# A two-layer decoder on one core: where a second group's norm stands in layer 0, and where the first root and the gathered sums stand in layer 1

## The chip, the cores and the metric

The kernel runs on one core of one Trainium2 chip. The metric is device time in microseconds (us), the median of three runs. A profile is one further execution, recorded by the hardware profiler.

The engines are called as the profile calls them: PE (TensorE, matmuls and transposes, with PEld for its weight loads), DVE (VectorE), ACT (ScalarE), POOL (GpSimd) and SP (SyncE, which here only issues transfers). Each engine works through its own queue in order and waits where an instruction needs another engine's result.

## What is computed

The reference is a decoder with two layers on 32 sequences of 100 tokens, 256 values a token. Each layer adds three blocks to the tokens, each behind a layer norm:

```python
x = x + _L0_attn_ref(_layernorm(x), Wq, Wk, Wv, Wo, bq, bk, bv, bo)   # causal softmax attention, 16 heads of 64
x = x + _L0_xattn_ref(_layernorm(x), ctx_512, ...)                    # cross attention to 361 context rows
x = x + _L0_ffn_ref(_layernorm(x), ...)                               # shared MLP + 8 experts, 2 per token
x = x + _L1_attn_ref(_layernorm(x), W1, b1, W2, b2)                   # causal attention without softmax, heads of 16
x = x + _L1_xattn_ref(_layernorm(x), ctx_512, ...)                    # cross attention, 16 heads of 64
x = x + _L1_ffn_ref(_layernorm(x), ...)                               # shared MLP + 64 experts, 8 per token

def _layernorm(x, eps=1e-5):
    m = mean(x); v = var(x)
    return (x - m) / sqrt(v + eps)
```

Everything is float32.

## The kernel before

The 3200 tokens lie in on-chip memory as 25 tiles of 128 tokens (`self.x`). A sequence is called a batch, so batch b holds tokens 100 b to 100 b + 99 and straddles tiles. The six blocks run one after the other, and each hands its successor normed tokens in transposed form (`self.xnT`).

**Queues.** PE's instructions stand in the order in which the program emits them (`tc.manual_schedule`). The queues of the other engines are ordered by a planner at build time, which may move an instruction ahead of others where its inputs allow it; `self.depend(got, [other], reason)` ties an instruction behind another one. All matmul results of the two attention blocks go to eight PSUM banks used in turn; a bank is free again once its result has been copied out.

**A norm** is made in groups of tiles. `norm_stats(f, groups)` (L163 on) takes the statistics of tile f (L175, L178); with the last tile of a group come the addition of epsilon (L180), the square root on ACT (L181) and the reciprocal on DVE (L182) for the whole group. `norm_rows` then forms the normed rows on DVE (L185), remembers the last one as `self.last_row`, and adds a bias to x on POOL (L200); `norm_turn` transposes them on PE (L207) and copies the result into `xnT`, by `evac`. `evac` (L124 on) counts its calls and sends each second copy to ACT (L128), the others to DVE (L129); its argument `act_of` changes the share: with 1, all go to ACT.

**Layer 0's attention.** SP loads the first tiles of x, then the weights wq and wk, then tiles 4 to 7, biases, wv, wo and the rest. `front(f)` norms and transposes a group (tiles 0 to 3, 4 to 7 and so on). `proj(b0, c, ...)` makes two of eight chunks of q (copied out with a scaled bias on ACT, L299) or k (DVE, L301) for two batches, `vals` the values of a batch in two halves. Then follow 64 steps, two a batch: scores, projections for the batches to come, the transposes of the step before, values. Scores are masked and reduced on DVE, exponentiated on ACT (L330) and scaled on POOL (L334).

**Layer 0's experts leave their rows in memory** (`y_d`). Layer 1 picks them up: `gather0(pool, f)` fetches two rows for each token of tile f by two indirect transfers, which POOL issues (L1252), into eight buffers `yk`, and adds each to x with its weight on DVE (L1257, "gathered sums" below). With `after` given, both sums stand behind that instruction.

**Layer 1's attention** begins with the gathers of tiles 0 to 3 and their statistics. To give PE work in the meantime, `ahead(steps, n)` makes keys and values of the cross attention that comes next (`keys1`: one step is two matmuls and two copies of 361 columns; `vals1`: a half of a batch is three of 512 columns); the text calls this the fill. The first group is tiles 0 to 3, the later ones three tiles each (FRONT1). Ahead of the loop stand the fill, the first two groups' norms and the projections of the first four batches. A step of the loop is one batch: `scores` (16 small matmuls in four banks, masked on DVE, L999), a projection, `vals` (L980), `values` of the batch before (L1009), the output projection of a finished tile (L237). In three of four steps a tile of a group to come is gathered and its statistics are taken; in the fourth the group is normed and transposed.

Of the kernel before, what the change touches and what calls it, by code (L numbers as in the profile page):

```python
# [12 lines left out]
AF = mybir.ActivationFunctionType  # L13
# [64 lines left out]
class Kernel:  # L78
    def __init__(self, ctx, tc, a):
        self.ctx, self.tc, self.nc, self.a = ctx, tc, tc.nc, a  # L80
        nc = tc.nc
        self.n_evac = 0
        self.const = ctx.enter_context(tc.tile_pool(name="const", bufs=1))
        self.wts = ctx.enter_context(tc.tile_pool(name="wts", bufs=1))
        self.lnp = ctx.enter_context(tc.tile_pool(name="ln", bufs=2))
        self.norms, self.norm_of = {}, {}
        self.x = self.const.tile([P, NF, D], F32, tag="x", name="x_sb")
        xd = a["x"].rearrange("b t d -> (b t) d").rearrange("(f p) d -> p f d", p=P)

        def load_x(f, n=4):  # L90
            n = min(n, NF - f)
            nc.sync.dma_start(self.x[:, f : f + n, :], xd[:, f : f + n, :])

        self.load_x = load_x
        load_x(0, 2)
        load_x(2, 2)
        self.xnT = self.const.tile([P, NK, NT], F32, tag="xnT", name="xnT")
        self.ident = self.const.tile([P, P], F32, tag="ident", name="ident")
        make_identity(nc, self.ident)
# [63 lines left out]
    def norm_stats(self, f, groups, after=None):  # L163

        nc = self.nc
        f0 = max(g for g in groups if g <= f)
        n, i = groups[f0], f - f0
        if i == 0:
            self.norm_of[n] = [
                self.lnp.tile([P, n, *k], F32, tag=f"{tag}{n}", name=tag)  # L170
                for tag, k in (("st", [6]), ("mv", [2]), ("rstd", []))
            ]
        st, mv, rstd = self.norm_of[n]
        self.norms[f] = mv[:, i, 0:1], rstd[:, i : i + 1]
        got = nc.vector.bn_stats(st[:, i, :], self.x[:, f, :])  # L175
        if after is not None:
            self.depend(got, [after.ins], "not ahead of the first tiles' norm")
        nc.vector.bn_aggr(mv[:, i, :], st[:, i, :])  # L178
        if i == n - 1:
            nc.vector.tensor_scalar_add(rstd, mv[:, :, 1], EPS)  # L180
            nc.scalar.activation(rstd, rstd, AF.Sqrt)  # L181
            nc.vector.reciprocal(rstd, rstd)  # L182

    def norm_row(self, f, out, eng):
# [55 lines left out]
    def l0_attn(self):  # L240
        nc, tc, a = self.nc, self.tc, self.a
        with ExitStack() as st:
# [34 lines left out]
            def front(f):  # L277

                n = FRONT0[f]
                for i in range(f, f + n):  # L280
                    self.norm_stats(i, FRONT0, self.last_row if f == 4 else None)
                for i in range(f, f + n, 2):
                    m = min(2, f + n - i)
                    self.norm_turn(i, m, self.norm_rows(i, m, bias=bo), self.bank_m())
# [18 lines left out]
            def vals(b, n):  # L303
                if n == 0:
                    v[b] = pool.tile([T, 1024], F32, tag="v", name="v", bufs=3)
                pm = self.bank_m()[:T, :]
                at = slice(n * 512, (n + 1) * 512)
                self.mm(pm, [(self.xn_of(i, b), wv[:, i, at]) for i in range(NK)])
                nc.vector.tensor_tensor(v[b][:, at], pm, bv[:T, at], ALU.add)
# [60 lines left out]

            with tc.manual_schedule(engines={mybir.EngineType.PE}):
                front(0)
                front(4)
                for c in range(0, 8, 2):
                    proj(0, c, wq, q, 0)
                    proj(0, c, wk, k, 1)
                for n in range(2):
                    vals(0, n)
                last = 2 * NB
                for n in range(last + 2):  # L380
                    b, g = divmod(n, 2)
                    if n < last:
                        scores(n)
                        b0 = b // 2 * 2 + 2
                        if b0 < NB:
                            c = 2 * (n % 4)
                            proj(b0, c, wq, q, 0)
                    if 0 < n <= last:
                        turn(n - 1)
                    if n < last and b0 < NB:  # L390
                        proj(b0, c, wk, k, 1)
                    if b + 1 < NB:
                        vals(b + 1, g)
                    if 0 < n <= last:
                        values(n - 1)
                    if g:
                        if b > 0:
                            out(b - 1)
                    elif b % 5 == 4 and b < 20:
                        front(4 * (b + 6) // 5)  # L400
                    elif later:
                        next_norm()
# [356 lines left out]
    def keys1(self, n):  # L759

        b, g = divmod(n, 4)
        t = self.k1[n] = self.kv.tile([P, 2, L], F32, tag="kT", name="kT", bufs=5)
        for j in range(2):
            c = 2 * g + j
            pm = self.bank_p()[:, :L]
            self.mm(pm, [(self.w1x[1][:, c * P : (c + 1) * P], self.ctx1[b][:, :L])])
            self.evac(t[:, j, :], pm)

    def vals1(self, b, half, c):

        if c == 0:
            self.v1[b, half] = self.kv.tile([KC, NKC, 512], F32, tag="v", name="v", bufs=4)
        t = self.v1[b, half, c] = self.v1[b, half]
        pm = self.bank_p()[:KC, :]
        wv = self.w1x[2]
        self.mm(pm, [(self.ctx1[b][:, c * KC : (c + 1) * KC], wv[:, half * 512 : (half + 1) * 512])])
        self.evac(t[:, c, :], pm)

    def l1_xattn(self):
        nc, tc, a = self.nc, self.tc, self.a  # L780
        self.route_begin()
        with ExitStack() as st:
# [97 lines left out]
                        )  # L880

            lay = Lay()
            self.xattn_stream(lay)


# [31 lines left out]
    def l1_attn(self):  # L917
        nc, tc, a = self.nc, self.tc, self.a
        with ExitStack() as st:
# [3 lines left out]
            pool = st.enter_context(tc.tile_pool(name="p1a", bufs=2))  # L923
            for f in range(FRONT1[0]):
                self.gather0(pool, f)
                self.norm_stats(f, FRONT1)
            keep = self.tri(cp, "keepT", 1, -1, 1.0, 0.0)

            row = cp.tile([P, 2], I32, tag="row", name="row")
# [106 lines left out]

            waiting = deque()

            halves = deque((b, half) for b in range(2) for half in range(2))

            def ahead(steps, n):
                for i in steps:
                    self.keys1(i)
                for _ in range(n):
                    b, half = halves.popleft()
                    for c in range(NKC):
                        self.vals1(b, half, c)

            with tc.manual_schedule(engines={mybir.EngineType.PE}):
                for i in range(2):  # L1050
                    for f in group(i):
                        if i > 0:
                            self.gather0(pool, f, self.last_row)
                            self.norm_stats(f, FRONT1)
                    f = group(i)[0]
                    if i == 0:
                        ahead(range(4), 3)
                    else:
                        ahead([], 1)
                    turn(f, 2)  # L1060
                    turn(f + 2, len(group(i)) - 2)
                    if i == 0:
                        ahead(range(4, 5), 0)
                    if i == 0:
                        for c in range(4):
                            proj(0, c)
                vals(0)
                for b in range(NB + 2):
                    i = b % 4
                    b0 = b - i  # L1070
                    if b < NB:
                        scores(b)
                    if b0 + 4 < NB:
                        proj(b0 + 4, i)
                    if b + 1 < NB:
                        vals(b + 1)
                    if 0 < b <= NB:
                        values(b - 1)
                    if b > 1:
                        out(b - 2)  # L1080
                    if b0 + 8 < NB:
                        fs = group(b0 // 4 + 2)
                        if i < 3:
                            self.gather0(pool, fs[i])
                            self.norm_stats(fs[i], FRONT1)
                        else:
                            turn(fs[0], 2)
                            turn(fs[2], 1)
                    if later:
                        later.popleft()()  # L1090
                    if waiting:
                        next_norm()
                while later:
                    later.popleft()()
# [890 lines left out]
```

## Time and profile before

| what | us |
|---|---|
| median of three runs (3193.65 to 3196.63) | 3195.87 |
| the profiled execution | 3204.05 |
| its span, first to last instruction | 3202.3 |
| PE busy in the span | 3067.3 (96%) |
| DVE busy | 1813.5 (57%) |
| ACT busy | 1393.2 (44%) |
| POOL busy | 925.7 (29%) |

The profile gives times from the span's start. Layer 0's attention begins at 0 and its first scores at 36.18; layer 1's attention has its first matmul at 1674.57, its first gather at 1678.74 and its first scores at 1718.68. In 1674 to 1850 PE is busy for 152.18 of 176 us at a mean granted clock of 0.88; in 1900 to 2100 for 198.44 of 200.

Busy time counts an engine's own instructions, not the time in which it waits. In a timeline line the first number is the start, the second the time it covers, and the bracket tells how long the engine had been idle and what ended that. A number after x at the line's end counts instructions; a float32 matmul appears as two.

### The profile page before, as it was taken

To read this page: it belongs to the slowest core of one execution; us is meant where nothing else is said; L and a number is where in the kernel's file an instruction comes from. 1 tells how busy PE (TensorE), PEld (TensorE's weight loads), DVE (VectorE), ACT (ScalarE), POOL (GpSimd) and SP (SyncE) were. 2 spreads that over 40 slices of the span, in tenths; PEclk is the share of its full clock that TensorE was granted. 3 is DMA by queue.
4 is the path that set the end of the run, shared out by engine and by line. 5 is a ranking of instruction groups with operands and counts; after the bars stand their busy time and mean duration, and the time that the engine had idled before them with its cause. 6 is when DMAs were issued, how large, how long until landed. Compare 5 with 4: busy or idle time off the path is not lost. (4 is left out here: it accounts for less than half of the span.)

```text
span 3202.3 us, 68027 instructions
## 1 busy us (share of the span) xinstructions
PE 3067.3 (96%) x26832; PEld 2231.9 (70%) x26832; DVE 1813.5 (57%) x4692; ACT 1393.2 (44%) x4346; POOL 925.7 (29%) x1048
## 2 busy tenths in 40 slices
PE   7999999999999999999997999999999999999983
PEld 6777777666666657888884667777777777776672
DVE  6666666566676732222226776666676666665443
ACT  4455554566656511222221225555555555455120
POOL 3222221455555542000007230011211112122474
PEclk9999999999999999999997999999999999999996
DMA  8840000000000033554542000010000000000487
GB/s 305 299 155 1 1 1 1 18 14 14 14 12 14 5 121 114 200 190 176 192 172 84 2 5 6 6 35 23 24 9 10 11 10 13 9 10 13 138 203 191
DMA packets 122456, 225.86 MB, mean 71 GB/s; under 512 B 40557, under 2 KB 98853, under 8 KB 115344
## 3 DMA queue, kind: packets, MB, share of 16 engines
q1 hardware_dynamic: 93616, 127.32, 12.3%
q0 software_dynamic: 27792, 90.81, 8.7%
q8 instruction: 215, 3.52, 0.5%
q10 hardware_dynamic: 720, 3.28, 0.2%
q14 instruction: 113, 0.93, 0.1%
HBM read 153.77 MB, written 113.61 MB: 83 GB/s over the span
## 5 line engine op out<-in xcount | busy, mean ns | idle before, releaser
L1643 POOL DMA_INDIRECT x_d<-xr,slot x200 | 194.4, 972 | 787.3 <-DVE kT L129 242.1
L440 ACT ACTIVATE wBx<-ps_t,m 100x361 f32<-100x361 f32 x512 | 281.3, 561 | 261.7 <-DVE m L437 238.6
L610 DVE TENSOR_REDUCE m<-ps_t 100x1 f32<-100x361 f32 x512 | 240.1, 526 | 109.6 <-PE ps_t L134 108.7
L134 PE MATMUL ps_t<-xnT,wA 128*128 128x200 f32 x1536 | 299.4, 339 | 0.6 <-DVE x_sb L237 0.6
L437 DVE TENSOR_REDUCE m<-ps_t 100x1 f32<-100x361 f32 x512 | 241.2, 526 | 80.0 <-PE ps_t L134 78.0
L134 PEld LDWEIGHTS ps_t<-xnT,wA 128*128 128x128 f32 x1536 | 259.0, 191 | 35.7 <-issue 17.9
L134 PE MATMUL ps_t<-xT,w 128*128 128x256 f32 x1276 | 283.2, 381 | 0.7 <-ACT xT L128 0.7
L134 PEld LDWEIGHTS ps_t<-xT,w 128*128 128x128 f32 x1276 | 240.0, 190 | 41.7 <-issue 9.3
L334 POOL TENSOR_TENSOR e<-e,rz 100x400 f32<-100x400 f32 x128 | 109.5, 856 | 414.0 <-DVE rz L333 397.1
L330 ACT ACTIVATE e<-s,m 100x100 f32<-100x100 f32 x512 | 186.4, 367 | 20.4 <-DVE m L324 20.1
L134 PE MATMUL ps_t<-wA,cT 128*121 128x512 f32 x384 | 187.3, 598 | 5.9 <-DVE mv L178 5.5
L631 ACT ACTIVATE e<-ps_t 121x300 f32<-121x300 f32 x512 | 173.4, 430 | 41.7 <-PE ps_t L134 41.6
L134 PE MATMUL ps_t<-kT,qT 64*100 64x361 f32 x1024 | 190.4, 489 | 0.9 <-ACT wBx L440 0.9
L134 PE MATMUL ps_t<-cT,wA 128*128 128x361 f32 x512 | 189.9, 495 | 1.3 <-DVEq L1243 1.3
L449 PEld LDWEIGHTS ps_t<-ident,wBx 100*121 100x121 f32 x1536 | 178.2, 186 | 12.9 <-issue 6.0
L134 PE MATMUL ps_t<-wA,zT 128*128 128x256 f32 x800 | 186.1, 386 | 0.4 <-issue 0.4
L449 PE MATMUL ps_t<-ident,wBx 100*121 100x100 f32 x1536 | 185.3, 270 | 0.0
L635 POOL TENSOR_TENSOR es<-e 121x400 f32<-121x400 f32 x128 | 132.8, 1038 | 177.6 <-ACT e L631 177.5
L1325 DVE TENSOR_TENSOR h<-ps_t,g 128x256 f32<-128x256 f32 x145 | 61.2, 424 | 199.4 <-ACT g L1324 199.4
L134 PEld LDWEIGHTS ps_t<-wA,zT 128*128 128x128 f32 x800 | 151.2, 192 | 29.2 <-issue 4.4
L129 DVE COPY eT<-ps_t 121x300 f32<-121x300 f32 x339 | 146.7, 461 | 31.2 <-PE ps_t L449 27.1
L467 PE MATMUL ps_z<-eT,v 121*64 121x100 f32 x3072 | 161.2, 254 | 0.8 <-issue 0.8
(300 smaller groups left out, 5790.2 us busy)
## 6 DMA issues: line engine op xcount, KB each, us to landing
x_d<-fill SPq DMA_DIRECT2D x16, 1284.0 KB
we<-in_wexp SPq DMA_DIRECT2D x32, 384.0 KB
cT<-in_ctxT SPq DMA_DIRECT2D x64, 181.5 KB
xe<-x_d SPq DMA_DIRECT2D x32, 321.0 KB
xe_d<-zero SPq DMA_DIRECT2D x8, 1024.0 KB
xe<-xe_d SPq DMA_DIRECT2D x29, 256.0 KB
y_d<-y SPq DMA_DIRECT2D x29, 256.0 KB
w_d<-in_wg SPq DMA_DIRECT2D x16, 320.0 KB
```

Of the source, the lines that this page charges most:

```text
L129: return self.nc.vector.tensor_copy(out, in_)
L134: self.nc.tensor.matmul(out, lhsT=l, rhs=r, start=(i == 0), stop=(i == n - 1))
L330: nc.scalar.activation(t[:, i, :], s[:, i, :], AF.Exp, bias=m[:, i : i + 1], accum_out=rz[:, i : i + 1])
L334: nc.gpsimd.tensor_tensor(t[:, h, :], t[:, h, :], self.last(rz[:, h], T), ALU.mult)
L437: lay.after = nc.vector.tensor_reduce(m, ps[i], AX.X, ALU.max, negate=True)
L440: nc.scalar.activation(t[:, :L], ps[i], AF.Exp, bias=m, accum_out=sums[b][:, h : h + 1])
L449: nc.tensor.transpose(pt[:, c, :], e[n, i][:, c * KC : (c + 1) * KC], self.ident[:T, :T])
L467: nc.tensor.matmul(out, lhsT=v, rhs=eT[n, i][:, c, :], start=first, stop=last)
L610: nc.vector.tensor_reduce(m[:, j, o : o + 1], ps[r], AX.X, ALU.max, negate=True)
L631: nc.scalar.activation(t[:, r], ps[r].rearrange("p (c t) -> p c t", c=NKC), AF.Exp)
L635: nc.gpsimd.tensor_tensor(s, t[:, :, 0, :], t[:, :, 1, :], ALU.add)
L1643: got = nc.gpsimd.indirect_dma_start(out=self.x1_d[:, :], out_offset=bass.IndirectOffsetOnAxis(ap=slot[:, j, k : k + 1], axis=0), in_=xr[: ...
```

## The change

In layer 0, `front(4)` moves from behind `front(0)` to behind the projections and values of the first batches.

In layer 1, three things change. The fill is emitted in one piece ahead of the first group's statistics, with five keys and four halves of values (before: four keys and three halves, then one key behind the first group's transposes and the last half ahead of the second group's), and all its copies go to ACT (`ahead_of` is 1 there, and 2 again in the cross attention). The first group's square root is tied behind the last of these copies (`norm_after`). And in the loop the gathered sums are tied behind the last norm row emitted until then (`self.last_row`), as those of the second group were already.

```diff
@@ norm_stats
         if i == n - 1:
             nc.vector.tensor_scalar_add(rstd, mv[:, :, 1], EPS)
-            nc.scalar.activation(rstd, rstd, AF.Sqrt)
+            got = nc.scalar.activation(rstd, rstd, AF.Sqrt)
+            if self.norm_after is not None:
+                self.depend(got, [self.norm_after.ins], "behind the fill's copies")
             nc.vector.reciprocal(rstd, rstd)
@@ l0_attn
                 front(0)
-                front(4)
                 for c in range(0, 8, 2):
                     proj(0, c, wq, q, 0)
                     proj(0, c, wk, k, 1)
                 for n in range(2):
                     vals(0, n)
+                front(4)
@@ keys1
-            self.evac(t[:, j, :], pm)
+            self.evac(t[:, j, :], pm, self.ahead_of)
@@ vals1
-        self.evac(t[:, c, :], pm)
+        return self.evac(t[:, c, :], pm, self.ahead_of)
@@ l1_xattn
             lay = Lay()
+            self.ahead_of = 2
             self.xattn_stream(lay)
@@ l1_attn
             for f in range(FRONT1[0]):
                 self.gather0(pool, f)
-                self.norm_stats(f, FRONT1)
...
+            self.ahead_of = 1
             halves = deque((b, half) for b in range(2) for half in range(2))
...
                     for c in range(NKC):
-                        self.vals1(b, half, c)
+                        got = self.vals1(b, half, c)
+                return got
...
+                    if i == 0:
+                        self.norm_after = ahead(range(5), 4)
+                        for f in group(0):
+                            self.norm_stats(f, FRONT1)
+                        self.norm_after = None
                     f = group(i)[0]
-                    if i == 0:
-                        ahead(range(4), 3)
-                    else:
-                        ahead([], 1)
                     turn(f, 2)
                     turn(f + 2, len(group(i)) - 2)
-                    if i == 0:
-                        ahead(range(4, 5), 0)
...
                         if i < 3:
-                            self.gather0(pool, fs[i])
+                            self.gather0(pool, fs[i], self.last_row)
                             self.norm_stats(fs[i], FRONT1)
```

More of the change, by code (lines that the diff above doesn't have):

```diff
@@ L85, in __init__ @@
         self.lnp = ctx.enter_context(tc.tile_pool(name="ln", bufs=2))
-        self.norms, self.norm_of = {}, {}
+        self.norms, self.norm_of, self.norm_after = {}, {}, None
         self.x = self.const.tile([P, NF, D], F32, tag="x", name="x_sb")
```

## The prediction

> **What bounds the kernel now.** I began with the page: TensorE (PE) is busy 96% of the 3202.3 us span, and in the windows by stage it is at 100% of 1900 to 2900 us. Its queue is written out by hand, so a microsecond in which PE stands idle early is a microsecond at the end. Then I read the waits of PE over the whole span, to see where the missing 4% lies.
>
> ```profile
> PE ps_t L207 <- DVE xn L185: 23.8, 7, 8.2
> PE ps_t L134 <- issue: 7.4, 17, 1.1
> PE ps_t L134 <- DVE mv L178: 5.5, 1, 5.5
> ```
>
> Columns: total us, times, longest. The largest wait is that of transposes (L207) for normed rows (L185), and two stages hold it. The first is the kernel's start, in the timeline:
>
> ```profile
> 8.04 0.69 DVE L129 COPY xnT<-ps_t 128x512 f32<-128x512 f32 x1 [0.23 <-PE ps_t L207]
> 14.10 0.75 DVE L175 BATCH_NORM_STATS2 st<-x_sb 128x6 f32<-128x256 f32 x2 [5.36 <-DMA x_sb<-in_x]
> 17.09 0.48 PE L207 MATMUL ps_t<-ident,xn 128*128 128x128 f32 x1 [8.23 <-DVE xn L185]
> 19.98 12.84 PE L134 MATMUL ps_t<-xnT,wA 128*128 128x200 f32 x64
> 36.18 0.95 PE L134 MATMUL ps_t<-qk,qk 64*100 64x100 f32 x16
> ```
>
> PE has the first group's rows transposed by 8.9 us, then waits 8.23 us for the second group, whose x only lands at 14.10. The projections at 19.98 need only the first group. The second place is the start of layer 1's attention:
>
> ```profile
> 1691.90 3.77 PE L134 MATMUL ps_t<-wA,cT 128*121 128x512 f32 x4 [5.54 <-DVE mv L178]
> 1693.38 0.21 ACT L181 ACTIVATE rstd<-rstd 128x4 f32<-128x4 f32 x1 [6.82 <-DVE mv L178]
> 1700.09 0.48 DVE L1257 SCALAR_TENSOR_TENSOR x_sb<-yk,wA,x_sb 128x256 f32<-128x256 f32 x1 [6.15 <-DMA yk<-y_d,wA]
> 1701.89 0.17 DVE L182 RECIPROCAL rstd<-rstd 128x4 f32<-128x4 f32 x1
> 1702.62 1.23 PE L207 MATMUL ps_t<-ident,xn 128*128 128x128 f32 x4 [6.95 <-DVE xn L185]
> ```
>
> Two waits. Copies of the fill (kT, v) stand in VectorE's (DVE's) queue behind sums of gathered rows, so no PSUM bank comes free: 5.54 us. Then the root is done at 1693.6, but its reciprocal stands behind two sums of a later tile that wait for their gather: 6.95 us. The windows show PE's granted clock fall to half here:
>
> ```profile
> 1692.00:1694.00 2.00, 2.00 (x3) 0.94 (x4) 1.94 (x6) 0.62 (x2) 1.70 (x2) 0.50 0.38 102
> 1706.00:1708.00 2.00, 2.00 (x5) 1.20 (x5) 1.66 (x4) 0.59 (x1) 1.79 (x2) 0.50 0.00 0
> ```
>
> (After the window: busy us of PE, weight loads, DVE, ScalarE (ACT), POOL; then clock, DMA share, GB/s.) Third, the loop behind it: scores (0) start at 1718.68 and scores (6) at 1771.83, 53.1 us for six batches, against 5.05 us each from 1766.65 to 1781.79, so 31 us undisturbed: 22 lost.
>
> **What the Trainium skill says.** "TensorE: Matmul & The Clock Gate", What's actually happening: an idle window of about 3.4 us halves the clock, a busy one restores it. Agreed: idle from 1686.4, 0.50 from 1690. "ScalarE: Activation LUTs", What ACT_TABLE_LOAD costs: 1283 ns; the trace has 1.28 us. "GPSIMD Engine Reference", Key points: POOL shares SBUF interfaces with VectorE; here norm rows take 0.40 us each at 1702.1 and 0.65 us at 1721.7 beside L200.
>
> **Part 1, layer 0: front(4) goes behind proj(0) and vals(0).** It moves eight transposes, two copies and their norm; SP's queue has the same order. PE can start once wq and wk have landed. Those landings aren't shown, so I bound them: both are issued ahead of the x load that lands at 14.10 (latest); 2.1 MB behind the first tiles (used at 4.68) at the 300 to 380 GB/s of the DMA row need 6 us (earliest 10.7). I take 12. The first projection (wq) runs in that wait. Evacuations wait for the scaled bias (L257, 14.77), but eight PSUM banks let PE run ahead. From the evacuations' pitch a projection takes 1.35 us warm: seven are 9.5, plus up to 1.7 for a cold clock; vals 3.5; the moved transposes 1.6. Scores (0) at 12 + 14.6 to 16.3 = 26.6 to 28.3, or up to 30.4 at a landing of 14.1, instead of 36.18: 6 to 9.5 gained. In the built order the roots of later fronts now fall between exps: two more pairs of table loads, 2 x 2.56 us on ACT, whose step has some 2 us of slack: up to 1 us each on PE, so I take 1 to 2. wv is issued by 9.6 us and its first use is now near 21 us: free. POOL's bias adds stay ahead of its first L334: no change. **Part 1: -7 us, from -3.5 to -9.**
>
> **Part 2, layer 1: the fill.** All five keys and four halves of vals now stand ahead of the first norm, 22 copies, all on ACT. PE: 10 x 0.64 (5.09 us for eight) + 12 x 0.86 = 16.7 us, from 1674.6 to 1691.3. ACT: 10 x 0.39 + 12 x 0.59 = 11.0 us, faster than PE, so the 5.54 us wait goes; what is queued behind the copies on ACT is only the root. DVE keeps sums and statistics: last sum at 1690.85, statistics by 1692. The root waits for the last copy (1692.1) and its table load, now uncovered: 1.28 us. Root 1693.6, first rows 1694.0, first transposes 1694.5 instead of 1702.62. The matmuls of two keys and three of vals (1.3 + 2.6 us) no longer follow the norm, but the first projections may still meet a cold clock (up to 3). Transposes and copies to 1697.6, projections 5.5 to 8, second group's transposes, vals: scores (0) near 1706.5, from 1704.5 to 1709, instead of 1718.68. **-12 us, from -9.5 to -14.**
>
> **Part 3: sums behind the norm in front.** Sums wait for the last emitted norm row (last_row); nothing is removed. POOL's queue becomes 16 gathers, 4 bias adds, then 6 gathers and 3 adds in turn; a gather costs 1.32 us of queue and lands 2.9 us after it starts (1678.74 to 1681.68). Gathers 17 to 22 run from about 1703 to 1711, behind the adds; so the sums ahead of scores (0)'s masking (L999) end near 1710.5 and L999 (0) near 1713 (before 1726.9). Adding the DVE entries of the built order, L999 (1) ends at 1718, (2) at 1724 (before 1746.6); from there 5.1 us a batch. Ideal: scores (6) at about 1739.5, 33 us after scores (0). But PE also lost time with nothing to wait for:
>
> ```profile
> 1738.68 1.05 PE L134 MATMUL ps_t<-qT,kT 32*100 32x100 f32 x5 [0.78 <-issue]
> 1766.65 0.96 PE L134 MATMUL ps_t<-qT,kT 32*100 32x100 f32 x32
> ```
>
> Scores (2) took 9.3 us instead of 0.96, likewise scores (4) and the end of (0), some 16 us together, each some us into an unbroken run of gathers. The trace doesn't say why. Those gathers are still to come: lower bound 0, upper bound the same 16; I take 7, since runs are now broken into sixes. Later groups carry their sums in the loop: 6 x 0.46 + 3 x 0.6 = 4.6 us of DVE per four batches, on a DVE that is busy 52.1 of 70 us at 1780 to 1850: 74% becomes 96%. PE may wait 0 to 2 us in each of four groups; I take 4 in all. Loop: 33 + 7 + 4 = 44 instead of 53: **-9 us, between +4 and -20.**
>
> Sum: -7 - 12 - 9 = -28; since the early rows of part 2 and the loop's first steps wait for the same gathers, I count 2 less: **-26 us.** The profiled execution took 3204.05 us (span 3202.3), 8.2 above the median of 3195.87; I take 26 from the median: 3170.
>
> **Rivals.** (a) *The issue stalls follow the gathers.* Parts 1 and 2 hold, the loop gains nothing: -16 to -19, about 3178. For it: 30 gathers are still to come in the loop in either kernel. Against: they come in sixes, and scores ran at full speed right after each pause. (b) *Layer 0 gives next to nothing*, as the weights land with x and table loads cost 3: about 3174, inside the range. (c) *Slower: DVE becomes the loop's bound.* If bias adds on POOL stretch DVE's rows (0.40 to 0.65 us) and sums block L999, each four batches overrun. With all 16 us of stalls kept, the loop's first six batches take 33 + 16 = 49 us, 4 less than now, and parts 1 and 2 give 19: it decides from (23 + 6) / 4 = 7 us a group, 40% more than DVE's 19.6 us per four batches; at 9 us it is +36 - 23 = +13, about 3209. Against: the deferred sums are needed a whole group later, so DVE can catch up. (d) *The root isn't earlier*: it was at 1693.38, and the copies put it at 1693.6. True; the gain must come from the reciprocal and the copies. If the planner's waits still delay the rows, part 2 shrinks to 5.
>
> **The numbers.** Main 0.72 ((b) and (d) with it), (a) 0.19, about no change 0.05 (that overrun at some 6 us a group), (c) 0.04. A measurement of this kernel tells about 0.2%, 6.4 us, from no change. Range: the main case's bounds run from -36 to -16, and (a) reaches to -13: 3158 to 3184.
>
> **What would show it.** Part 1: PE's first 128x200 projection near 9, its run from 12, scores (0) at 27 to 30. Part 2: no 5.5 us gap in the fill, no DVE copy of kT or v there, rows near 1694 less part 1's gain. Part 3: no DMA wait between root and reciprocal; "issue" waits of PE in the loop tell main case and (a) apart. Scores (0) to (6) over 53 us in layer 1 would prove part 3 wrong; scores (0) of layer 0 later than 33 us, part 1.

## The result, and the profile after

The changed kernel takes **3173.91 us** (median of four runs, 3168.08 to 3178.49) against 3194.76 us for the kernel before beside it (3193.29 to 3196.63, four runs): a ratio of 0.9933, 95% interval 0.9916 to 0.9951, some 21 us. Its profiled execution took 3178.49 us, with a span of 3176.8; the span before was 3202.3.

In the changed file the lines of the two norms and of the gathers stand a little lower: L182, L185, L207, L999, L1252 and L1257 are now L184, L187, L209, L1001, L1256 and L1261. First the waits of PE over the whole span (total us, times, longest):

```profile
PE ps_t L209 <- DVE xn L187: 10.2, 3, 6.7
...
PE ps_t L134 <- DVE s L1001: 3.1, 2, 2.0
```

Transposes waiting for normed rows are down from 23.8 to 10.2 us. "Issue" (a gap for which the profile shows nothing that PE waited for) is no longer among the large waits; in its place comes a smaller one, scores that wait until the masking (L1001) has freed their banks. The timeline of the kernel's start after the change:

```profile
6.66 1.99 PE L209 MATMUL ps_t<-ident,xn 128*128 128x128 f32 x8 [6.66 <-DVE xn L187]
10.51 13.52 PE L134 MATMUL ps_t<-xnT,wA 128*128 128x200 f32 x64 [1.87 <-DMA wA<-in_wq]
14.60 0.75 DVE L175 BATCH_NORM_STATS2 st<-x_sb 128x6 f32<-128x256 f32 x2 [6.07 <-DMA x_sb<-in_x]
27.30 1.04 PE L209 MATMUL ps_t<-ident,xn 128*128 128x128 f32 x8
28.27 0.95 PE L134 MATMUL ps_t<-qk,qk 64*100 64x100 f32 x16
```

Projections start at 10.51 instead of 19.98, behind a wait of 1.87 us for wq. The second group's x still lands late (14.60), but its transposes at 27.30 no longer wait for it. The first scores start at 28.27 instead of 36.18. The start of layer 1's attention, same view:

```profile
1674.52 10.46 PE L134 MATMUL ps_t<-wA,cT 128*121 128x512 f32 x24
...
1685.02 0.59 ACT L128 COPY v<-ps_t 121x512 f32<-121x512 f32 x1 [0.27 <-PE ps_t L134]
...
1687.38 0.20 ACT L181 ACTIVATE rstd<-rstd 128x4 f32<-128x4 f32 x1
1687.62 0.18 DVE L184 RECIPROCAL rstd<-rstd 128x4 f32<-128x4 f32 x1 [1.61 <-ACT rstd L181]
...
1688.39 1.99 PE L209 MATMUL ps_t<-ident,xn 128*128 128x128 f32 x8 [3.41 <-DVE xn L187]
1689.26 0.88 DVE L1261 SCALAR_TENSOR_TENSOR x_sb<-yk,wA,x_sb 128x256 f32<-128x256 f32 x2
...
1691.26 7.39 PE L134 MATMUL ps_t<-xnT,wB 128*128 128x400 f32 x16 [0.87 <-DVE xnT L129]
```

The values of the fill run as one unbroken row of 24 matmuls, and ACT copies one each 0.86 us, waiting 0.27 us each time for PE, not PE for it. Reciprocal follows root at once, and the next tiles' sums (1689.26) come behind the normed rows. The windows there (busy PE, weight loads, DVE, ACT, POOL; then clock):

```profile
1688.00:1690.00 2.00, 1.61 (x8) 1.54 (x8) 1.96 (x6) 0.43 (x1) 1.39 (x3) 0.51 0.24 68
...
1692.00:1694.00 2.00, 2.00 (x4) 1.01 (x3) 1.96 (x7) 0.00 (x0) 1.68 (x3) 0.50 0.30 96
```

The halved clock is still there: the wait of 3.41 us for the normed rows is left, and behind it the first transposes and projections run at half the clock, as before. And in the loop:

```profile
1717.64 2.00 DVE L1001 TENSOR_TENSOR s<-ps_t,keepT 100x400 f32<-100x400 f32 x4
...
1718.25 2.61 PE L134 MATMUL ps_t<-qT,kT 32*100 32x100 f32 x30 [1.97 <-DVE s L1001]
...
1720.80 3.04 PE L134 MATMUL ps_t<-xnT,wB 128*128 128x400 f32 x4
...
1728.03 0.96 PE L134 MATMUL ps_t<-qT,kT 32*100 32x100 f32 x32
```

Scores (3) wait 1.97 us for the masking, and the projection behind them takes 3.04 us instead of 1.61, at a clock of 0.50. This is the one large loss left there: 12.2 us from scores (3) to (4), where undisturbed batches take about 5.

Where the 25 us between the two profiled spans came from, as lead over the kernel before at the same instruction: 7.9 at layer 0's first scores, 6.2 at layer 1's first matmul (1668.38 against 1674.61), 18.6 at layer 1's scores (0) (1700.10 against 1718.68), 33.2 at scores (6) (1738.59 against 1771.83), 26.7 at the cross attention's first scores (1885.43 against 1912.08), 25.5 at the end. These are two single executions; which part of the lead the edit made is for the experiments to tell.

### The profile page after: what moved, and what is told of

Its sections match the earlier page's. It is cut to its first block, busy times and chain, and to the rows that moved or that the text cites. A ratio compares the mean times of both kernels' runs of the same rounds, so it can differ in the third digit from the quotient of the medians.

```text
span 3176.8 us, 68045 instructions
## 1 busy us (share of the span) xinstructions
PE 3058.3 (96%) x26832; PEld 2230.1 (70%) x26832; DVE 1811.6 (57%) x4681; ACT 1402.8 (44%) x4361; POOL 928.7 (29%) x1048
## 5 line engine op out<-in xcount | busy, mean ns | idle before, releaser
L332 ACT ACTIVATE e<-s,m 100x100 f32<-100x100 f32 x512 | 186.1, 364 | 21.1 <-DVE m L326 20.4
L469 PE MATMUL ps_z<-eT,v 121*64 121x100 f32 x3072 | 161.1, 254 | 0.0
## 6 DMA issues: line engine op xcount, KB each, us to landing
xe_d<-zero SPq DMA_DIRECT2D x8, 1024.0 KB, 16.3
```

The source lines that it names most:

```text
L332: nc.scalar.activation(t[:, i, :], s[:, i, :], AF.Exp, bias=m[:, i : i + 1], accum_out=rz[:, i : i + 1])
L469: nc.tensor.matmul(out, lhsT=v, rhs=eT[n, i][:, c, :], start=first, stop=last)
```

## The experiments

The runs were made on three chips: the first four kernels on one where the kernel before takes 3205.2 us, the next four on one with 3207.66, the last four on one with 3196.92. Ratios are to the kernel before on the same chip, and "us under before" below is worked out from the ratio. On which chip the two profiles of before and after were taken is not on record. The stages below are read from the timeline of each one's profile, in us: from the fill's first matmul to the first transposes (A) and to scores (0) (B), scores (0) to (6), scores (6) to (31), and PE's issue waits from 1665 to 1910. "Tied" and "free" say whether the loop's sums stand behind the norm row in front.

| kernel | A | B | (0)-(6) | (6)-(31) | issue | ratio, 95% interval |
|---|---|---|---|---|---|---|
| before | 28.0 | 44.1 | 53.1 | 128.0 | 7.6 | 1 |
| e5, before again | 27.9 | 44.4 | 50.7 | 128.1 | 6.3 | 0.9992 (0.9983 to 1.0001) |
| after | 20.0 | 31.7 | 38.5 | 134.6 | 0 | 0.9933 (0.9916 to 0.9951) |
| e9, after again | 20.7 | 32.9 | 36.7 | 134.5 | 0 | 0.9929 (0.9916 to 0.9942) |
| e1, layer 0 alone | 28.5 | 45.0 | 54.8 | 128.7 | 10.7 | 0.9977 (0.9968 to 0.9985) |
| e2, layer 1 alone | 20.2 | 32.6 | 42.4 | 138.2 | 4.9 | 0.9959 (0.9941 to 0.9976) |
| e3, fill alone | 40.4 | 56.8 | 47.9 | 128.0 | 7.4 | 1.0013 (1.0005 to 1.0021) |
| e4, sums alone | 21.4 | 33.9 | 37.6 | 141.1 | 4.3 | 0.9964 (0.9949 to 0.9979) |
| e6, first group tied | 20.3 | 31.6 | 58.3 | 129.5 | 9.0 | 0.9962 (0.9948 to 0.9975) |
| e7, root free | 22.7 | 40.0 | 38.1 | 139.2 | 5.9 | 0.9964 (0.9953 to 0.9976) |
| e8, copies shared | 23.2 | 38.6 | 41.6 | 142.1 | 6.5 | 0.9971 (0.9960 to 0.9982) |
| e10, two groups tied | 20.5 | 33.5 | 48.0 | 134.0 | 0 | 0.9958 (0.9945 to 0.9970) |
| e11, three groups tied | 20.4 | 31.7 | 52.6 | 131.5 | 0 | 0.9977 (0.9966 to 0.9987) |
| e12, no loop gathers | 20.7 | 35.4 | 36.3 | 128.0 | 0 | one run |

The issue waits need a warning before any two rows are compared. In the stretch of the table nine profiles have them (before, e1 to e8), five have none (after, e9 to e12). The same nine, and only they, also have three such gaps in a row at the end of layer 1's cross attention, which no edit touches (line L467, or L469 in the changed file). In the kernel before, from 2951 us on:

```profile
PE ps_z L467 <- issue: 0.8, 3, 0.3
```

These three are 0.8 to 1.0 us in e1 to e8 and absent in the other five, although all have POOL's indirect transfers some 1.3 us apart there. So whether a profile has issue waits goes with the group of runs it belongs to: every kernel on the first two chips has them, tied or not, and none on the third, tied or not. The profile of before (3204.05 us) is as long as the kernel before takes on the first two chips, its timed runs (3195.87) as on the third. Where a row with issue waits stands beside one without, the difference need not be the edit's alone; that holds for the rows before and after, too.

### The parts alone: e1 to e4

**e1**, the kernel before with only `front(4)` moved behind `vals(0, n)`:

> Only front(4) is moved behind the first projections and values; layer 1 is as before. My theory (parts add up): layer 0's first scores about 8 us earlier than 36.18, layer 1's first fill matmul 6 us earlier, the time 5 to 7 us under before (about 3189). Rival (the gain of layer 0 is only phase: the slack comes back in layer 1's start, where gathers and fill decide): first fill matmul 6 us earlier, but time within 2 us of before.

3197.31 us, 0.23% or 7.4 us under its chip's kernel before, a little more than the theory's 5 to 7; layer 0's first scores at 27.81, the fill's first matmul at 1668.05. The part pays by itself and nothing in layer 1 takes it back.

**e2**, all of layer 1's edits and layer 0 as before:

> All of layer 1's changes, front(4) where it was before. Theory: 15 to 19 us under before (about 3178), start of the loop 12 us earlier than before, its first six batches 10 to 15 us shorter, later batches some 6 us longer. Rival (the issue stalls of the profiled execution of before are not in the timed runs): start 12 us earlier, loop equal, 10 to 13 us under before.

3190.48 us, 0.41% or 13 us, at the upper end of the rival's 10 to 13 and short of the theory's 15 to 19, though the interval (8 to 19) takes in both. In its profile the start (B) is 11.5 us shorter, the first six batches are 10.7 shorter and the later ones 10.2 longer: the loop as a whole, 180.6 us, takes as long as before (181.1). With e1 that makes 0.64%, against 0.67% for both together: within the intervals the two layers add up.

**e3**, as e2, but without the tie of the sums in the loop:

```diff
-                            self.gather0(pool, fs[i], self.last_row)
+                            self.gather0(pool, fs[i])
```

> Layer 1's fill in one piece with its copies on ACT and the first root behind them, but the loop's gathered sums left free; layer 0 as before. Theory: the 5.5 us wait in the fill goes; the free sums still stand ahead of the reciprocal and keep 6 us of its wait, so 5 to 8 us under before. Rival (the planner itself puts the sums behind the norm once the copies are off VectorE): no DMA wait between root and reciprocal, 12 us or more under before.

3209.88 us: the fill's edits alone make the kernel 0.13% slower, which neither expectation allowed for. The timeline tells why:

```profile
1693.09 0.20 ACT L181 ACTIVATE rstd<-rstd 128x4 f32<-128x4 f32 x1
1699.53 0.48 DVE L1261 SCALAR_TENSOR_TENSOR x_sb<-yk,wA,x_sb 128x256 f32<-128x256 f32 x1 [7.82 <-DMA yk<-y_d,wA]
...
1712.96 0.48 DVE L1261 SCALAR_TENSOR_TENSOR x_sb<-yk,wA,x_sb 128x256 f32<-128x256 f32 x1 [0.91 <-DMA yk<-y_d,wA]
1713.37 0.17 DVE L184 RECIPROCAL rstd<-rstd 128x4 f32<-128x4 f32 x1
...
1714.19 1.13 PE L209 MATMUL ps_t<-ident,xn 128*128 128x128 f32 x4 [23.76 <-DVE xn L187]
```

The root is done at 1693.3, but the planner has put eight free sums between root and reciprocal in DVE's queue, and these wait for their gathers: the reciprocal comes 20 us behind the root. PE's wait grows to 23.76 us.

**e4**, the reverse: the kernel before with only that tie.

> Only the loop's gathered sums are tied behind the last norm row; fill, copies and layer 0 as before. Theory: the 6.9 us wait of the first transposes goes, the 5.5 us wait in the fill stays; with a shorter start of the loop and 6 us lost in later batches 5 to 10 us under before. Rival (VectorE is full in the loop and the deferred sums cost as much as they save): within 2 us of before or slower.

3193.29 us, 0.36% or 11.6 us: nearly all of layer 1's gain, and a little more than the 5 to 10 expected. The fill still has its hole, but the norm no longer stands behind gathers:

```profile
1695.95 3.77 PE L134 MATMUL ps_t<-wA,cT 128*121 128x512 f32 x4 [5.61 <-DVE mv L178]
...
1697.44 0.21 ACT L181 ACTIVATE rstd<-rstd 128x4 f32<-128x4 f32 x1 [6.89 <-DVE mv L178]
...
1699.52 1.92 PE L207 MATMUL ps_t<-ident,xn 128*128 128x128 f32 x8
```

The hole of 5.61 us is as long as before, but the transposes come 2 us behind the root instead of 9. Of the 12.4 us that the change takes off stage B, the tie alone brings 10.2; the fill adds 2.2 to it and, without the tie, costs 12.7. The loop behind it gains little: 178.7 us from scores (0) to (31), against 181.1 before and 178.9 in e5.

### Repetition, and one edit undone at a time: e5 to e8

**e5**, the kernel before as it is:

> The kernel before, unchanged, profiled once more. Theory (the stalls of PE with nothing to wait for belong to unbroken runs of gathers): 12 us or more of them again in the first six batches of layer 1's loop, scores (0) to (6) about 53 us. Rival (they are chance, and the profiled execution of before was simply a slow one, 8 us over its median): under 4 us of them, scores (0) to (6) some 40 to 45 us.

The waits of PE between 1665 and 1765 again hold issue:

```profile
PE ps_t L134 <- issue: 4.6, 11, 1.1
PE ps_t L1009 <- issue: 1.7, 3, 0.9
```

So the stalls of the loop recur, in other batches and of another size, and six batches again take over 50 us. The sum of 6.3 us lies between the theory's 12 and the rival's 4, so neither is confirmed.

**e6**, the change with the tie in the loop's first group only (`self.last_row if b0 == 0 else None`):

> The changed kernel, but only the sums gathered in the first four batches are tied; those of later groups are free. Theory (the 6.6 us that the changed kernel loses after batch 6 come from sums and gathers spread over later batches, as each group waits for the norm ahead of it): later sums go early again and the later batches take 3 to 7 us less, while batches 2 to 6 take as much more; time within 3 us of the changed kernel. Rival (the tie of later groups costs and its removal is free): 4 to 6 us faster than the changed kernel. Second rival (free sums push into the first steps): 5 us slower or more.

```profile
1707.58 3.15 DVE L1261 SCALAR_TENSOR_TENSOR x_sb<-yk,wA,x_sb 128x256 f32<-128x256 f32 x5 [6.60 <-DMA yk<-y_d,wA]
...
1711.21 3.01 PE L134 MATMUL ps_t<-xnT,wB 128*128 128x400 f32 x4 [7.84 <-DVE xnT L129]
```

The freed sums of later groups moved forward and waited 6.60 us for a gather, with a copy of xnT behind them on DVE and a projection behind that. The first six batches take 58.3 us, far more than was expected; the later ones come back to 129.5. The ratio, 0.9962 against 0.9933 for the change on another chip, speaks for the second rival.

**e7**, the change with the root not tied behind the fill's copies (`norm_after` stays `None`):

> The changed kernel without the tie of the first root behind the fill's copies. Theory: the planner puts the root's table load and the root among the copies as before; the root still needs the statistics (1692 less 6 us), so copies behind it on ACT wait and PE loses up to 2 us in the fill, but the table load of 1.28 us is hidden: within 2 us of the changed kernel. Rival (the tie is what matters): a root early in ACT's queue blocks the copies until the last statistics, banks run full, 4 us slower or more.

```profile
1675.82 1.28 ACT L181 ACT_TABLE_LOAD   x1
1685.62 0.20 ACT L181 ACTIVATE rstd<-rstd 128x4 f32<-128x4 f32 x1 [8.53 <-DVE x_sb L1261]
...
1686.36 4.53 PE L134 MATMUL ps_t<-wA,cT 128*121 128x512 f32 x6 [4.31 <-ACT v L128]
```

Left free, the root goes ahead of most copies in ACT's queue and waits 8.53 us there for its statistics; the copies pile up behind it and PE waits 4.31 us for a bank, then 6.24 us ahead of the projections. Stage B takes 40.0 us instead of 31.7: the rival, not the theory.

**e8**, the change with the fill's copies shared between ACT and DVE (`self.ahead_of = 2`):

> The changed kernel with the fill's copies shared between ACT and VectorE again. Theory (a copy on VectorE stands behind sums that wait for their gathers): PE waits 3 to 6 us in the fill, 3 to 6 us slower than the changed kernel. Rival (the one-piece fill alone does it, since the sums of later tiles no longer stand ahead): within 1.5 us of the changed kernel.

```profile
1674.98 1.98 PE L134 MATMUL ps_t<-wA,cT 128*121 128x512 f32 x4 [0.96 <-DVE kT L129]
...
1695.72 7.49 PE L134 MATMUL ps_t<-xnT,wB 128*128 128x400 f32 x16 [4.13 <-DVE xnT L129]
```

Copies on DVE again stand behind sums: five waits in the fill, 3.1 us together, and 4.13 us for the copy of xnT. Stage B: 38.6 us. So with the sums tied the fill's edits work only as a whole: without the root's tie or without the copies on ACT, stage B is 5 to 6 us longer than with none of the fill's edits (e4, 33.9). The profiles of e6 to e8 also hold issue waits in the loop (5.9 to 9.0 us), and the change itself was not run on their chip.

### The change again, fewer ties, no gathers: e9 to e12

**e9**, the change unedited:

> The change itself, unedited, on the chip on which the experiments ran, so that they can be held against it. Theory (the ratio carries over, and first projections and sums add up): front alone gave -8, layer 1 alone -14 to -15 here, so about -22 (3185). Rival (the loop's first six batches were short in the first profile by luck, since every other kernel with tied sums shows issue waits there): scores(0) to scores(6) of layer 1 nearer 43 to 46 us than 38.5, issue waits of 3 to 5 us on TensorE, and -15 to -17 (3191), no better than the kernels with one piece undone.

3174.22 us, ratio 0.9929: the gain and the stages repeat, with no issue wait. It ran on the third chip, though, where none of e1 to e8 ran and no kernel has issue waits in the loop. So it doesn't tell whether the change keeps its short loop where the others have these waits, which was its rival's question.

**e10** and **e11** free the sums from the third or the fourth group of the loop on (`self.last_row if b0 <= 4 else None`, and `<= 8`):

> The change with the gathered sums tied to the norm in front in the first two groups of the loop only (b0 of 0 and 4), free from the third on. Theory (the tie pays where gathers are late, and costs where VectorE has to run the sums between the masking steps of later batches): batches after scores(6) give back the 5 to 7 us that they lost against the kernel before, first six within 3 us of the whole change: 4 to 6 us under it, about 3180. Rival (as with only the first group tied: free sums are placed early and wait for their gathers with the masking behind them): first six or the next batches lose 8 to 20 us, 3190 or more.

> As the kernel with two groups tied, but three groups tied (b0 of 0, 4 and 8). Theory: scores(6) to (31) lose only what batches 4 to 11 lose, 2 to 3 us of the 6; about 3 us under the whole change, 3183, and first six batches as in it. Rival: the free sums of the fourth group wait for late gathers ahead of the masking of batches 8 to 12: a DMA wait of VectorE there and no gain, 3186 or more.

3185.73 and 3190.53 us: both are slower than the change (0.9929 on the same chip), and the rival holds. e10's timeline:

```profile
1715.50 0.48 DVE L1261 SCALAR_TENSOR_TENSOR x_sb<-yk,wA,x_sb 128x256 f32<-128x256 f32 x1 [6.92 <-DMA yk<-y_d,wA]
...
1717.86 0.39 PE L134 MATMUL ps_t<-qT,kT 32*100 32x100 f32 x2 [4.46 <-DVE rstd L184]
1721.81 2.61 PE L134 MATMUL ps_t<-qT,kT 32*100 32x100 f32 x30 [3.56 <-DVE s L1001]
```

and e11's, where it comes later:

```profile
1730.46 0.48 DVE L1261 SCALAR_TENSOR_TENSOR x_sb<-yk,wA,x_sb 128x256 f32<-128x256 f32 x1 [6.18 <-DMA yk<-y_d,wA]
...
1732.95 1.56 PE L1011 MATMUL ps_t<-s,v 100*32 100x100 f32 x32 [5.84 <-DVE v L982]
```

A free sum stands early in DVE's queue and waits 6 to 7 us there, with masking and copies behind it. The later batches get cheaper by 0.5 and 3.0 us, but the first six lose 11.3 and 15.9 (both against e9). These three profiles are of one chip and without issue waits, so this is the clean measure of what free sums cost in the loop.

**e12**, the kernel before without the gathers that the loop issues (36 of them; their sums read a tile of zeros):

> The kernel before, with the 36 gathers that are issued inside layer 1's loop left out: their sums are still computed, from a tile of zeros, so part of layer 1's input is missing. Theory (TensorE's issue waits and VectorE's late masking in the first batches both come from runs of gathers): no issue waits between 1718 and 1772, scores(0) to scores(6) in 31 to 35 us instead of 51 to 53, span about 18 us shorter. Rival (the instructions of this stretch come late for another reason): issue waits of 5 us or more stay in the same batches, and the six take 40 us or more.

3180.73 us in one run, 16 under the kernel before. No issue wait is left, and the six batches take 36.3 us. They don't reach the 31 to 35 us; that fits DVE's windows, which are full for a while (DVE is the third figure):

```profile
1721.00:1725.00 4.00, 3.31 (x44) 2.04 (x42) 4.00 (x14) 1.63 (x5) 0.00 (x0) 1.00 0.02 4
1725.00:1729.00 4.00, 3.99 (x66) 2.79 (x66) 4.00 (x12) 0.59 (x1) 0.00 (x0) 1.00 0.00 0
```

The time says what gathers and the waiting for them cost the kernel before in all: some 16 us. The profile can't say how that divides. That issue waits are absent proves nothing about gathers, as e9 to e11 on the same chip have none either with all gathers in place, and neither has e12 at the indirect transfers of the cross attention, which it keeps. So of the 17 us between the six batches of before and of e12, up to the 16 that the prediction counts for stalls may be what sets the two groups of runs apart, not the gathers; stage A, where before shows no issue wait, is 7 us shorter. The change keeps every gather, moves what waits for them, and comes within about 2 us of this kernel in both places.

## Why the prediction was right

The predicted 3170 is 4 us under the 3173.9 measured. The gain is 21 us, not 26. Parts 1 and 2 came about as described, although their credit lay elsewhere than it was put; that part 3 gained what was counted is not shown, and some of the agreement is luck.

**Part 1** (-7): -6.2 in the profile at layer 1's first matmul, -7.4 by e1. (Single executions differ by some 5 us ahead of that matmul, as e9 has it at 1673.54; over all fourteen profiles the mean is 6.3 earlier with the part than without.) Scores (0) at 28.27 lie in the predicted 26.6 to 28.3. Two terms were off. The landing was taken as 12, with wq's projection running in the wait near 9: PE waited for wq itself, and could start everything at 10.51, just ahead of the earliest bound of 10.7. And eight projections took 13.5 us, 1.7 each, not 1.35 and a cold clock. The table loads came as counted, seven from 8 to 115 us where there were three. Of 7.9 us at the scores 1.7 are gone by the fill, inside the 1 to 2 set aside for them; that the loads are the cause was not tested.

**Part 2** (-12): -12.4. Less part 1's 6.2 us, root, first transposes and scores (0) were predicted at 1687.4, 1688.3 and 1700.3; they start at 1687.38, 1688.39 and 1700.10. The root came no earlier after the fill's start (19.0 us, before 18.8), as rival (d) said, and the gain lay in the reciprocal and the copies. The failing step is the credit: "DVE keeps sums and statistics" and rows at 1694.0 suppose that no other sum stands between root and reciprocal, which is part 3's edit. By e3 and e4, part 2 alone would have been a loss, and the tie alone most of the gain.

**Part 3** (-9): not confirmed. In the two profiles the lead grew from 18.6 to 26.7 us over the loop, 8.1. But one of them has issue waits and the other none. In the timed runs little is left for the loop: 21 us less the 7.4 of e1 and the 12.4 of part 2 is 1 us, by e9's 22.7 it is 3, and the interval of either is 4 us or more to each side. Where all profiles have issue waits, scores (0) to (31) take 177 to 184 us with all sums tied (e2, e4, e7, e8) and 176 to 184 with them free (before, e1, e3, e5). Where none has, they take 171.2 tied (e9) and 182 to 184 with only two or three groups tied (e10, e11); the kernel before, with all free, has no profile there.

Of the terms 33 + 7 + 4, issue stalls, taken as 7, were 0 in both profiles of the change and 4 to 6.5 us in the four tied kernels named. The first six batches had 38.5 us all the same: 5.5 over the 33, mostly scores (3) waiting for the masking and the half clock behind it. And later batches lost 6.6 us (134.6 against 128.0), not 4; in the four kernels they lost 10 to 14. The windows and the timeline of the change, around scores (17):

```profile
1752.00:1822.00 70.00, 68.34 (x941) 47.10 (x940) 60.23 (x161) 19.10 (x50) 38.74 (x42) 1.00 0.07 21
```

```profile
1798.85 2.09 DVE L1261 SCALAR_TENSOR_TENSOR x_sb<-yk,wA,x_sb 128x256 f32<-128x256 f32 x3
1800.86 2.00 DVE L1001 TENSOR_TENSOR s<-ps_t,keepT 100x400 f32<-100x400 f32 x4
...
1802.03 1.83 PE L134 MATMUL ps_t<-qT,kT 32*100 32x100 f32 x32
```

DVE is busy 60.2 of 70 us (86%, not the 96% worked out), but three sums in a row push one masking back by 2.1 us, and the next scores take 1.83 us instead of 0.96. The average hid that; here it was the order within a batch that cost time.

**The sum** (-26): the profiles differ by 26.7 us at the end of the loop, but the times by 21. The mis-sized term is part 3, with the step "I take 26 from the median": the losses of the loop were read from an execution 8 us over its median, and that of the change was 4.6 over its own. The 7.6 us of issue waits in it would account for the 8, if the timed runs of before had none; no profile of such a run was taken. Two readings don't come out of the figures shown, and nothing turns on them: six batches of 5.05 us are 30.3, not 31, and the bounds of the three parts add up to -41 to -7 with the 2 taken off, not -36 to -16.

Rivals: (a), that parts 1 and 2 hold and the loop gains nothing (-16 to -19, about 3178), is not ruled out. Its reason, stalls that follow the gathers, doesn't show in the change's profiles, but its time lies inside the interval of the measured gain (15.7 to 26.8 us), and e2 fits it. On the third chip e9's interval (18.5 to 26.9) leaves it only its upper end. (b) is out by e1; (c) by the lead, which shrank by 6.6 us behind scores (6), not by 36. A DVE that blocks the loop did come, in e6, e10 and e11, where sums were left free, not where they were tied.

## What to carry to other kernels

Before an engine's queue is filled with work that waits for a slow transfer, look at what stands behind that work: here one tie, which removed nothing, was worth 11 us, and edits that freed the engine in front were a loss without it. Edits whose credit seems separate may share one wait, so each is worth a run alone. Tie late work consistently: leaving the later groups free cost 11.5 and 16.3 us (e10 and e11, against e9). And before a difference between two profiles is laid to an edit, look at a stretch that the edit doesn't touch: here three small gaps there tell which profiles may be compared.

## What the runs showed that was not expected

**Behind a gap of 2 us PE's clock was halved.** In the change PE had nothing from 1716.28 to 1718.25, and the windows show a clock of 0.50 from 1719 to 1725; two of them (the clock is the third figure from the end):

```profile
1717.00:1718.00 1.00, 0.00 (x0) 0.00 (x0) 0.96 (x3) 0.24 (x2) 0.84 (x3) 1.00 0.00 0
...
1719.00:1720.00 1.00, 1.00 (x19) 0.92 (x21) 1.00 (x5) 0.39 (x3) 0.81 (x1) 0.50 0.36 90
```

"TensorE: Matmul & The Clock Gate", What's actually happening, in the Trainium skill, speaks of an idle window of about 3.4 us; in this trace less was enough, and the slow stretch cost more (3.04 instead of 1.61 us for one projection, and 1.91 instead of 1.03 for the values behind it) than the gap.

**PE has gaps for which the profile gives no reason.** They last up to 1.4 us and add up to 4 to 11 us of layer 1's first attention in before and e1 to e8. They lie beside runs of indirect transfers, there and at the end of the cross attention, but such transfers are not sufficient: the change issues gathers 1.32 us apart in sixes with no such wait, and in five profiles the unedited cross attention has the transfers without the gaps. What sets the two groups of runs apart, the chip or something else, stays open. "Runtime: NRT & Kernel Launch", Instruction fetch mechanics, says that an engine's instructions come by DMA in blocks and that this is mostly hidden; delayed fetches would fit what is seen, but no run measured them.
